# ScalarE's casts of sources and values behind the Gelu of the messages, and another order of small steps at the end of layer 0

## The chip, the cores and the metric

The kernel runs on one core of one Trainium2 chip. The metric is the device time of one execution in microseconds (us), the median of the runs given. TensorE is called PE here (PEld its weight load), VectorE DVE, ScalarE ACT, GpSimd POOL, and SyncE, which only issues DMAs, SP. A line number such as L1012 is a line of the kernel before.

## The reference

A graph of N = 2708 nodes with D = 128 features each passes through four layers; each takes h = relu(layernorm(x)) and adds its result to x. The adjacency matrix adj is 2708 x 2708 in f32, with about 0.6% of its entries not zero and the diagonal set.

- Layer 0: x + (adjᵀ h) / (column sums of adj).
- Layer 1: messages between nodes, `aggregated[i] = sum over j of gelu(s[i] + d[j] + msg_b) * adj[i, j]`, with s and d two linear images of h; then a dense update with a Gelu, and a layernorm.
- Layer 2: adj h through a linear map and a GRU cell.
- Layer 3: two heads of masked attention over adj's entries, with their own layernorms.

The change touches the end of layer 0 and layer 1.

## The kernel before

Nodes are cut into 22 tiles of 128 rows (NT = 22, the last one of 20 rows), and a matrix row into 22 blocks of 128 columns (NB = 22). Each engine works through its instructions in the order of the code: the order is written by hand, there is no planner. The kernel issues, for each part, a short function for one step of the work, and the order of the calls is what the change edits.

**Layer 0.** The matrix is read in pieces of 512 columns (a cut, `c`, 0 to 5; LAST is 5) by sets of four row tiles (`s`, 0 to 5). For each piece PE sums adjᵀ h, ACT and PE also turn the piece over for a later layer, and DVE lists, for each block of 128 columns of a row, its eight largest entries and where they are (`list_cut`, MAX8 and FIND_INDEX8 in L356 and L358). These lists, `val` and `col`, are the edges of layer 1. The columns of the last cut are done by parts between the sets of cut 4 (`PARTS`). Steps of the column sums of cut c-1 run during cut c (`next_steps`): `lift`, `spread`, `sum_rows`, `sum_squares`, `normal_rows` are generators, of which `work_cut` takes one step at a time between its matmuls. Behind them the rows of h for layer 1 are made: `turn_rows`, `destinations` (d by PE), `take_lead` and `split_rest` (d cut into three bf16 parts, d3, by ACT, DVE and POOL), `invert`, `add`, `measure`, `rows`.

**Layer 1.** It computes messages only for listed entries, at most 128 per block and row tile. For tile `t` and block b, PE makes the arguments of the Gelu by two sums of three bf16 matmuls each (`combine`, L1012 and L1016): a choice of source rows, `sel` (a 0/1 matrix), times the parts of s (s3), plus a choice of columns, `cols`, times d3. ACT applies Gelu to 4 blocks of p_m at once (`activate`, L1024; p_m has two buffers, g three), and PE sums the results into the rows of the tile with a third matrix, `put` (`gather`, L1037, f32). A tile is one `period(t)` of six steps, k = 0 to 5, with one combine and one activate each; gathers of 8 blocks at k = 3 and 5, and of the rest at k = 1 of the next period.

While tile t is computed, its successors are prepared:
- tile t + 3: `rank` (PE: where each row's entries begin), `spread_ends`, `lead_of` (ACT, L568: first bf16 part of the values, into `xb`), `select_rows` (DVE: sel), `describe_rest` (L946: the rest `v_r` on DVE, its cast on ACT, L572, the third part and two copies on POOL), `finish_rows` (DVE, L625: sel minus sel shifted by a DMA, `later`);
- tile t + 2: `fetch` (PE, L639), `place` (DVE: value and column of each listed entry), `find_rows` (DVE: `mine`, L601);
- tile t + 1: `pass_on` and `spread_columns` (two DMAs on SP), `columns` (DVE: cols, L973), `put_values` (POOL, eight blocks) and `put_more` (ACT, L965, the other fourteen blocks in parts).

In every even period before the last, the two source tiles that come next are made: `project` (PE), `add_bias` (DVE: sb, L728), `take_sources` (ACT, L568: first part of s), and `sources_rest` (L991: the rest `s_r` on DVE, its cast on ACT, L572, the third part on POOL, a Gelu and two scalings on ACT). `mix` and `update` do the dense part for groups of four tiles in between.

Period 0 takes its preparation from the lists `opening` and the `run` ahead of it. Buffers that the steps name: `hot` and `picked` are scratch tiles of one buffer each, `xb` has two, by the parity of t.

Of the kernel before, what the change touches and what calls it, by code (L numbers as in the profile page):

```python
# [20 lines left out]
F32 = mybir.dt.float32  # L21
# [9 lines left out]
P = 128  # L31
# [29 lines left out]
def listed_layers(ctx: ExitStack, tc: tile.TileContext, x, adj, w, out, flag):  # L61
# [204 lines left out]
    def sum_squares(g):  # L266
        t, k = GROUPS[g]
        for q in range(t, t + k):
            junk = pool.tile([P, D], F32, name="junk")
            nc.scalar.activation(  # L270
                junk, xs[:, q, :], AF.Square, bias=flat[:, 0, q : q + 1], accum_out=flat[:, 1, q : q + 1]
            )
            if q == t + k - 1:
                shift, ve, rstd, tmp = (flat[:, r, t : t + k] for r in range(4))
                nc.gpsimd.tensor_scalar(ve, ve, 1.0 / D, EPS, ALU.mult, ALU.add)
                nc.gpsimd.tensor_tensor(rstd, ve, minus_half[:, 0:k], ALU.pow)
                nc.gpsimd.tensor_tensor(tmp, rstd, rstd, ALU.mult)
                nc.gpsimd.tensor_tensor(tmp, tmp, ve, ALU.mult)
                nc.gpsimd.tensor_scalar(tmp, tmp, -0.5, 1.5, ALU.mult, ALU.add)
                nc.gpsimd.tensor_tensor(rstd, rstd, tmp, ALU.mult)  # L280
                nc.gpsimd.tensor_tensor(shift, shift, rstd, ALU.mult)
            yield
# [167 lines left out]
    def turn_sums(g):  # L450

        t, k = GROUPS[g]
        p = sums_p[g] = bank("p_s0")
        for q in range(k):
            m = size(t + q)
            nc.tensor.transpose(p[0:m, q * P : (q + 1) * P], sums_T[g][:, q * P : q * P + m], ident)
# [59 lines left out]
    def next_steps(c, s):  # L516

        off = 1 if c < LAST - 1 else 0
        stage = s - 1 - off
        if stage == -1:  # L520
            return lift(c - 1)
        if stage == 0:
            return spread(c - 1)
        if stage == 1:
            return sum_rows(c - 1)
        if stage == 2:
            return sum_squares(c - 1)
        if stage == 3:
            return normal_rows(h, c - 1)
        return last_destinations() if stage == 4 and c == LAST - 1 else ()  # L530

    def last_destinations():
        destinations(LAST - 2)
        yield
        pass_on(0)
        project(0)
        turn_sums(LAST)
        yield

    def list_last(n):  # L540
# [41 lines left out]

    def less_lead(t):
        dst, src = values_of(t)
        rest = state["x", t] = opener.tile([P, NB, S], F32, name="hot")
        nc.vector.tensor_tensor(rest, src, dst[0], ALU.subtract)

    def pass_rest(t):
# [144 lines left out]
    for i, (c, s) in enumerate(order):  # L733
        g0, gk = GROUPS[s]
        list_cut(c, s, g0)
        if i == 0:
            state["f", 0] = factors(*state.pop(("m", -1)))
            list_cut(c, s, g0 + 1)
            state["m", 1] = moments(tiles_of(xs, *GROUPS[1]), "n4")
            list_cut(c, s, g0 + 2)  # L740
            state["f", 1] = factors(*state.pop(("m", 1)))
            list_cut(c, s, g0 + 3)
        else:
            for n in range(g0 + 1, g0 + gk):
                if c > 0 and s == (2 if c < LAST - 1 else 1) and n == g0 + 1:
                    invert(c - 1)
                list_cut(c, s, n)
            if c == LAST - 1:
                for n in {0: range(FIRST), 1: range(FIRST, 4), 2: range(4, HELD), LAST: range(NT - 2, NT)}.get(s, ()):
                    list_last(n)  # L750
                if s == 0:
                    count_some(0, FIRST)
                if s == 1:
                    count_some(FIRST, 1)
        if i + 1 < len(order):
            mask_near(*order[i + 1])
        if i > BEHIND and i - 1 - BEHIND + RING < len(order):
            load_cut(*order[i - 1 - BEHIND + RING])
        for z in {(LAST - 2, 3): (0,), (LAST - 2, 4): (1,), (LAST - 2, 5): (2,), (LAST - 1, 0): (3,), (LAST - 1, 2): (4,), (LAST - 1, 3): (5,)}.get(
            (c, s), ()  # L760
        ):
            load_cut(LAST, z)
        if (c, s) == (LAST - 1, 2):
            shift_rows(0)
        if c > 0 and s == (2 if c < LAST - 1 else 1):
            turn_sums(c - 1)
        if (c, s) == (LAST - 1, LAST):
            turn_rows(LAST - 2)
        work_cut(c, s, first_steps(s) if c == 0 else next_steps(c, s))
        if c > 1 and s == 3:  # L770
            split_rest(c - 2)
        if (c, s) == (LAST - 1, 3):
            pass_rest(0)
        if c > 1 and s == 0:
            turn_rows(c - 2)
        if c > 1 and s == 1:
            destinations(c - 2)
        if c > 1 and s == 2:
            take_lead(c - 2)
        if c == LAST - 1:  # L780
            if s == 1:
                ranked = rank(0, FIRST, bank("p_r"))
            for z in PARTS.get(s, ()):
                mask_near(LAST, z)
                work_cut(LAST, z)
            if s == 1:
                nc.vector.tensor_copy(*ranked)
                spread_ends(0)
                select_rows(0)
                lead_of(*values_of(0))  # L790
            if s == 2:
                less_lead(0)
                finish_rows(0)
            if s == 3:
                for q in range(2):
                    fetch(0, q)
            if s == LAST - 1:
                place(0)
                lead_of(*values_of(2))
                less_lead(2)  # L800
                for _ in lift(LAST):
                    pass

        if (c, s) == (1, 2):
            nc.sync.dma_start(msg_wT, w["msg_wT"])
        if (c, s) == (2, 3):
            nc.sync.dma_start(msg_b, w["msg_b"].partition_broadcast(P))
            nc.gpsimd.tensor_copy(src_self[:, 0, :], msg_wT[:, 0, :])
            nc.gpsimd.tensor_tensor(src_self[:, 1, :], msg_wT[:, 0, :], msg_wT[:, 1, :], ALU.add)

    write_one()

    pass_rest(2)
    lead_of(*values_of(1))
    take_lead(LAST - 2, pool.tile([P, 4, D], F32, bufs=1, name="part_x"))
    add(LAST)
    measure(LAST)
    less_lead(1)
    add_bias(0, d_rest.rearrange("p (t c) d -> p t c d", t=2))
    spread_ends(1)  # L820
    split_rest(LAST - 2)
    for _ in lift(LAST - 1):
        pass
    turn_sums(LAST - 1)
    rows(LAST)
    pass_rest(1)
    ending.close()
    l0.close()

# [31 lines left out]
    with (  # L861
# [82 lines left out]
                    )  # L944

        def describe_rest(t):  # L946
            rest_of(*values_of(t), once.tile([P, NB, S], F32, name="v_r"))
            describe_columns(t)

        def put_values(t):  # L950

# [25 lines left out]
        def sources(k):  # L977

            sb = once.tile([P, 2, 2, D], F32, name="sb")
            if k not in projected:  # L980
                project(k)
            add_bias(k, sb)
            take_sources(k)

        def take_sources(k):

# [140 lines left out]
        def period(t, opening):  # L1127
# [6 lines left out]
            for k in range(GB):  # L1134
# [3 lines left out]
                if k == 0 and c and begun:  # L1138
                    pass_on(t + 1)
                    spread_columns(t + 1)  # L1140
                if k == 1 and a:
                    nc.vector.tensor_copy(*rank(t + 3, 1, rpool.tile([P, CH], F32, tag="r", name="p_r")))
                    spread_ends(t + 3)
                if k == 1 and last:
# [23 lines left out]
                if k == 2:  # L1168
                    if now and t % 2 == 0 and t + 2 < NT:
                        sources(t // 2 + 1)  # L1170
                    if a and begun:
                        select_rows(t + 3)
                        describe_rest(t + 3)
                    if now and t % 2 == 0 and t + 2 < NT:
                        sources_rest(t // 2 + 1)
                    if now and t + 4 < NT - 2:
                        count_rows(t + 4)
                if k == 1 and t == NT - 2:
                    check_lists()
                if k > 0 and c and begun:  # L1180
# [12 lines left out]
                if k == 4 and a and not begun:  # L1193
                    select_rows(t + 3)
                    describe_rest(t + 3)
                if k == (4 if begun else GB - 1) and a:
                    finish_rows(t + 3)
                if k in (0, 3):
# [24 lines left out]
        def take_pair(g):  # L1223
# [6 lines left out]
        )  # L1230
        opening = {
            1: ((turn_rows, 4), (fetch_both, 1), (select_rows, 2), (put_more, 0, 1)),
            2: ((destinations, 4), (put_more, 0, 2), (put_more, 0, 3), (place, 1), (take_lead, 4), (finish_rows, 2)),
            3: ((split_rest, 4), (pass_on, 1), (spread_columns, 1), (put_more, 0, 4), (put_more, 0, 5)),
            4: ((fetch_both, 2), (find_rows, 1), (put_values, 1)),
            5: ((place, 2),),
        }
# [880 lines left out]
```

## Time and profile before

| what | value |
|---|---|
| three runs | 983.99, 986.82, 988.04 us, median 986.82 |
| profiled execution | 986.58 us, span 984.8 us |
| mean granted TensorE clock of the profiled execution | 0.968 |
| PE, DVE, ACT, POOL busy (share of the span) | 93%, 81%, 54%, 45% |
| layer 0 | 0 to about 200 us |
| layer 1 | about 201 to 544 us |
| layers 2 and 3 | from there to the end |

Busy time is the time in which an engine executed something. The profile also tells what ended each idle time of an engine: `PE p_m L1012 <- ACT g L1024` says that PE, before the matmul of line 1012 that writes p_m, waited for ACT's instruction of line 1024. Times in the timeline count from the span's start.

### The profile page before, as it was taken

How to read it: one execution, taken by the hardware profiler on the slowest of the kernel's cores; microseconds unless marked ns; L12 is line 12 of the kernel's file. 1: busy time of each engine (PE TensorE's matmuls, PEld its weight loads, DVE VectorE, ACT ScalarE, POOL GpSimd, SP SyncE). 2: the span in 40 equal slices, each digit the busy share in tenths (PEclk: the TensorE clock that was granted, in tenths of full speed). 3: DMA queues.
4: the chain of work that ended last, by engine and by line, in shares of the span. 5: the costliest groups of instructions: out<-in, count | busy, mean ns of one | idle time of the engine just before them, and what ended most of it. 6: DMA issues, size and time to landing. Idle time of an engine off the chain costs nothing. (4 is left out here: it accounts for less than half of the span.)

```text
span 984.8 us, 21973 instructions
## 1 busy us (share of the span) xinstructions
PE 911.1 (93%) x7948; PEld 742.5 (75%) x7948; DVE 797.0 (81%) x2753; ACT 531.8 (54%) x1561; POOL 444.1 (45%) x524
## 2 busy tenths in 40 slices
PE   6799999768999999899999999999789999999983
PEld 3465556558999999898999444444678999999972
DVE  7999999788988989889674756566689877997793
ACT  5766776656666756676566123433222553655242
POOL 5402221369976787969765634444111300430132
PEclk9999999978999999999999899999899999999996
DMA  9899998325543434323215355564301674456000
GB/s 334 286 354 365 359 368 296 125 94 160 169 129 117 149 115 135 120 81 132 91 62 190 119 190 208 194 237 134 93 6 57 211 245 151 145 186 208 1 17 15
DMA packets 81736, 163.61 MB, mean 166 GB/s; under 512 B 9100, under 2 KB 27056, under 8 KB 81618
## 3 DMA queue, kind: packets, MB, share of 16 engines
q1 hardware_dynamic: 62518, 129.98, 40.8%
q10 hardware_dynamic: 19100, 32.13, 9.0%
q8 instruction: 64, 1.05, 0.5%
q14 instruction: 54, 0.44, 0.1%
HBM read 115.47 MB, written 30.87 MB: 149 GB/s over the span
## 5 line engine op out<-in xcount | busy, mean ns | idle before, releaser
L1327 PE MATMUL att<-hv,wt 128*128 128x129 f32 x1672 | 195.7, 278 | 7.9 <-DVE wt L1297 6.4
L956 POOL TENSOR_SCALAR put<-count,line,value 128x128 f32<-128x128 f32 x176 | 197.6, 1134 | 11.1 <-DVE value L673 10.4
L1327 PEld LDWEIGHTS att<-hv,wt 128*128 128x128 f32 x1672 | 191.9, 194 | 10.9 <-DVE wt L1297 8.9
L1016 PE MATMUL p_m<-d,cols 128*128 128x128 bf16 (+1 forms) x1452 | 162.6, 221 | 9.2 <-DVE cols L973 4.3
L1012 PE MATMUL p_m<-s,sel 128*128 128x128 bf16 x1452 | 162.4, 221 | 5.0 <-ACT g L1024 4.9
L1297 DVE SCALAR_TENSOR_TENSOR wt<-row,lift,mask 128x1024 f32<-128x1024 f32 (+1 forms) x132 | 138.8, 1083 | 22.2 <-PE att L1327 22.2
L121 POOL TENSOR_TENSOR n_r<-n_r,minus_half 128x4 f32<-128x4 f32 (+1 forms) x28 | 38.9, 1389 | 237.7 <-DVE n_r L120 236.0
L1037 PE MATMUL agg<-put,g 128*128 128x128 f32 (+1 forms) x968 | 126.8, 284 | 0.0
L1037 PEld LDWEIGHTS agg<-put,g 128*128 128x128 f32 x968 | 116.2, 196 | 2.4 <-issue 0.2
L388 PE MATMUL sums<-a,h 128*128 128x512 f32 x220 | 113.9, 613 | 1.6 <-ACT h L137 1.6
L1488 PE MATMUL p_agg<-a,hs 128*128 128x512 f32 (+2 forms) x264 | 108.8, 554 | 2.8 <-DMA a<-adjT 2.8
L1012 PEld LDWEIGHTS <-sel 128*128 128x128 bf16 x1452 | 103.9, 99 | 9.0 <-issue 8.3
L1016 PEld LDWEIGHTS <-cols 128*128 128x128 bf16 (+1 forms) x1452 | 101.9, 99 | 10.1 <-DVE cols L973 5.0
L1024 ACT ACTIVATE g<-p_m 128x512 f32<-128x512 f32 x132 | 72.7, 552 | 63.8 <-PE agg L1037 45.0
L403 PEld LDWEIGHTS p_T<-ident,a 128*128 128x128 f32 (+1 forms) x440 | 55.4, 144 | 60.7 <-issue 43.1
L965 ACT ACTIVATE put<-mine,value 128x128 f32<-128x128 bf16 x308 | 100.6, 392 | 0.0
L358 DVE FIND_INDEX8 col<-val,a 128x8 uint16<-128x128 f32 x327 | 91.6, 298 | 0.0
L410 ACT ACTIVATE aT<-p_T 128x512 f32<-128x512 f32 (+2 forms) x132 | 71.1, 541 | 27.5 <-PE p_T L403 26.6
L1488 PEld LDWEIGHTS p_agg<-a,hs 128*128 128x128 f32 (+1 forms) x264 | 47.5, 193 | 50.6 <-issue 46.3
L403 PE MATMUL p_T<-ident,a 128*128 128x128 f32 (+1 forms) x440 | 70.5, 281 | 11.9 <-DMA a<-in_adj 6.2
L1450 ACT ACTIVATE hs<-hs 128x1354 f32<-128x1354 f32 (+1 forms) x44 | 58.5, 1330 | 39.9 <-DMA hs<-in_adj 39.5
L356 DVE MAX8 val<-a 128x8 f32<-128x128 f32 x327 | 79.4, 289 | 0.0
(297 smaller groups left out, 1529.0 us busy)
## 6 DMA issues: line engine op xcount, KB each, us to landing
hs<-in_adj SPq DMA_DIRECT2D x42, 677.0 KB
adjT<-aT ACTq DMA_DIRECT2D x50, 512.0 KB
a<-adjT SPq DMA_DIRECT2D x20, 1280.0 KB
a<-in_adj SPq DMA_DIRECT2D x24, 1024.0 KB
spread<-passed SPq DMA_DIRECT2D x22, 704.0 KB
later<-sel SPq DMA_DIRECT2D x22, 616.0 KB
cols_a<-in_adj SPq DMA_DIRECT2D x11, 320.0 KB
row<-own_d ACTq DMA_DIRECT2D x10, 256.0 KB
```

The costliest lines, as they stand in the source:

```text
L356: nc.vector.max(val[0:m, n, b, :], v)
L358: nc.vector.max_index(col[0:m, n, b, :], val[0:m, n, b, :], v)
L388: nc.tensor.matmul(accs[c][:, 0:w], h0[0:m, n, :], a[0:m, n - g0, t0 * P - lo : t0 * P - lo + w], start=(n == 0), stop=(n == NT - 1),)
L403: nc.tensor.transpose(p[0:k, i * iw + q * P : i * iw + q * P + m], a[0:m, q, e : e + k], ident[0:m, 0:m])
L956: nc.gpsimd.tensor_scalar(st["put", 0][:, b, :], count, st["line"][:, b : b + 1], st["value"][:, b : b + 1], ALU.is_equal, ALU.mult,)
L965: nc.scalar.activation(st["put", 1][:, b - HP, :], st["mine"][:, b - HP, :], AF.Identity, scale=st["value"][:, b : b + 1])
L1012: nc.tensor.matmul(p[:, b - b0, :], st["sel"][:, b, :], s3[:, q, t % 2, :], start=(q == 0), stop=False)
L1016: nc.tensor.matmul(p[:, b - b0, :], st["cols"][0:kb, b, :], d3[0:kb, b, q, :], start=False, stop=(q == 2))
L1037: nc.tensor.matmul(agg, g[:, b - 4 * k, :], put, start=(b == 0), stop=False)
L1297: nc.vector.scalar_tensor_tensor(wt[:, 0:n], row[:, k, c : c + n], lift[:, j, k : k + 1], mask[:, j, c : c + n], op0=ALU.max, op1=ALU.mult,)
L1327: nc.tensor.matmul(banks[s // 3][:, s % 3, :], wt[:, q * P : (q + 1) * P], hv[:, j, k, :], start=(v < 2 and s // 3 not in touched), stop=( ...
L1488: nc.tensor.matmul(pa[:, 0:n], h[0:k, j, :], a[0:k, j - j0, 0:n], start=(j == 0), stop=(j == NT - 1))
```

## The change

All edits move steps; the arithmetic stays the same.

- Cut 4, the last that is read whole: tiles 0 to 3 of the last cut's list are listed and counted at set 0 (before: three there, the fourth at set 1), tile 4 is counted at set 2, and the rank of four tiles is computed at once (p_r of 88 columns instead of 66), so period 0 computes none. The remainder of the values of tile 0 (`pass_rest(0)`) is issued ahead of the squares in set 3 (before: behind that set). `project(0)` and the first casts of the values of tiles 2 and 1 (`lead_of`) are steps of set 4. `turn_rows` of cut 3 comes between the last two parts of the last cut, `destinations` of cut 3 and `pass_on(0)` ahead of set 5. `less_lead(2)`, `less_lead(1)`, `spread_ends(1)` and `add_bias(0)` come directly behind `place(0)`; the rest of tile 1 uses a part of the scratch tile `picked`. `pass_rest(2)`, `pass_rest(1)` and `turn_sums(LAST)` are steps of set 5.
- Period 0: `split_rest(4)` comes in step 2 and `finish_rows(2)` in step 3 (before: the other way round). `take_sources(1)` and `sources_rest(1)` come at the end of steps 3 and 4.
- All later periods: `describe_rest` does only the subtraction on DVE in step 2. The cast of the rest on ACT and POOL's three instructions (`pass_rest`) come in step 3, behind `activate(t, 3)`. In even periods `take_sources` comes in step 3 behind that Gelu (before: step 2), and `sources_rest`, with its subtraction on DVE, in step 4 behind `activate(t, 4)`, so on DVE behind `columns`, `place` and `find_rows` of step 3.

```diff
@@ next_steps
         if stage == 2:
-            return sum_squares(c - 1)
+            squares = sum_squares(c - 1)
+            return in_turn(in_order((pass_rest, 0)), squares) if c == LAST - 1 else squares
         if stage == 3:
-            return normal_rows(h, c - 1)
-        return last_destinations() if stage == 4 and c == LAST - 1 else ()
-
-    def last_destinations():
-        destinations(LAST - 2)
-        yield
-        pass_on(0)
-        project(0)
-        turn_sums(LAST)
+            last = c == LAST - 1
+            return in_turn(in_order((project, 0), (lead_of, *values_of(2)), (lead_of, *values_of(1))), normal_rows(h, c - 1)) if last else normal_rows(h, c - 1)
+        if stage == 4 and c == LAST - 1:
+            return in_order((pass_rest, 2), (pass_rest, 1), (turn_sums, LAST))
+        return ()
+
+    def in_order(*steps):
+
+        for step, *numbers in steps:
+            step(*numbers)
         yield
...
@@ less_lead
-        rest = state["x", t] = opener.tile([P, NB, S], F32, name="hot")
+        if t == 1:
+            rest = opener.tile([P, NB, 4, S], F32, name="picked").rearrange("p b q s -> p (b q s)")[:, 0 : NB * S]
+            rest = rest.rearrange("p (b s) -> p b s", s=S)
+        else:
+            rest = opener.tile([P, NB, S], F32, name="hot")
+        state["x", t] = rest
...
@@ the sets of layer 0
-                for n in {0: range(FIRST), 1: range(FIRST, 4), 2: range(4, HELD), LAST: range(NT - 2, NT)}.get(s, ()):
+                for n in {0: range(FIRST + 1), 2: range(4, HELD), LAST: range(NT - 2, NT)}.get(s, ()):
                     list_last(n)
                 if s == 0:
                     count_some(0, FIRST)
-                if s == 1:
                     count_some(FIRST, 1)
+                if s == 2:
+                    count_some(FIRST + 1, 1)
...
         if (c, s) == (LAST - 1, LAST):
-            turn_rows(LAST - 2)
+            destinations(LAST - 2)
+            pass_on(0)
         work_cut(c, s, first_steps(s) if c == 0 else next_steps(c, s))
...
-        if (c, s) == (LAST - 1, 3):
-            pass_rest(0)
...
-                ranked = rank(0, FIRST, bank("p_r"))
+                ranked = rank(0, FIRST + 1, bank("p_r"))
             for z in PARTS.get(s, ()):
                 mask_near(LAST, z)
                 work_cut(LAST, z)
+                if z == LAST - 1:
+                    turn_rows(LAST - 2)
...
                 place(0)
-                lead_of(*values_of(2))
                 less_lead(2)
+                less_lead(1)
+                spread_ends(1)
+                add_bias(0, d_rest.rearrange("p (t c) d -> p t c d", t=2))
...
-    pass_rest(2)
-    lead_of(*values_of(1))
     take_lead(LAST - 2, pool.tile([P, 4, D], F32, bufs=1, name="part_x"))
     add(LAST)
     measure(LAST)
-    less_lead(1)
-    add_bias(0, d_rest.rearrange("p (t c) d -> p t c d", t=2))
-    spread_ends(1)
     split_rest(LAST - 2)
...
-    pass_rest(1)
@@ layer 1
         def describe_rest(t):
-            rest_of(*values_of(t), once.tile([P, NB, S], F32, name="v_r"))
-            describe_columns(t)
+            dst, src = values_of(t)
+            rest = state["x", t] = once.tile([P, NB, S], F32, name="v_r")
+            nc.vector.tensor_tensor(rest, src, dst[0], ALU.subtract)
...
@@ sources
             add_bias(k, sb)
-            take_sources(k)
...
@@ period
+                if k == 1 and a and not begun:
+                    spread_ends(t + 3)
-                if k == 1 and a:
+                elif k == 1 and a:
...
-                    if now and t % 2 == 0 and t + 2 < NT:
-                        sources_rest(t // 2 + 1)
-                    if now and t + 4 < NT - 2:
+                    if now and begun and t + 4 < NT - 2:
                         count_rows(t + 4)
+                even = now and t % 2 == 0 and t + 2 < NT
+                if k == 3 and a and begun:
+                    pass_rest(t + 3)
+                if k == 3 and even:
+                    take_sources(t // 2 + 1)
+                if k == 4 and even:
+                    sources_rest(t // 2 + 1)
...
+                if k == GB - 1 and a and not begun:
+                    pass_rest(t + 3)
...
@@ opening
-            2: ((destinations, 4), (put_more, 0, 2), (put_more, 0, 3), (place, 1), (take_lead, 4), (finish_rows, 2)),
-            3: ((split_rest, 4), (pass_on, 1), (spread_columns, 1), (put_more, 0, 4), (put_more, 0, 5)),
+            2: ((destinations, 4), (put_more, 0, 2), (put_more, 0, 3), (place, 1), (take_lead, 4), (split_rest, 4)),
+            3: ((finish_rows, 2), (pass_on, 1), (spread_columns, 1), (put_more, 0, 4), (put_more, 0, 5)),
```

`in_turn` takes the steps of several generators one after the other.

## The prediction

> **What bounds the kernel now.** I read first where the two touched stretches lie, in the busy time of each engine by stretch (columns: start and end, length, busy us and instructions of PE, PEld, DVE, ACT, POOL, then granted TensorE clock, DMA share, GB/s):
>
> ```profile
> core 0: us, PE busy (x) PEld busy (x) DVE busy (x) ACT busy (x) POOL busy (x), PEclk, DMA share, GB/s
> 175.00:190.00 15.00, 11.40 (x77) 7.83 (x76) 10.24 (x57) 8.99 (x39) 5.94 (x18) 0.89 0.34 128
> 190.00:205.00 15.00, 8.87 (x39) 4.81 (x38) 12.76 (x49) 9.34 (x31) 5.47 (x10) 0.79 0.39 127
> 205.00:222.00 17.00, 13.11 (x176) 12.00 (x177) 14.62 (x26) 9.93 (x30) 13.01 (x13) 0.88 0.14 44
> 222.00:545.00 323.00, 314.17 (x4377) 305.07 (x4376) 265.90 (x782) 210.40 (x639) 245.68 (x255) 0.98 0.40 126
> 393.00:409.00 16.00, 13.51 (x183) 12.99 (x182) 15.42 (x54) 11.05 (x35) 15.61 (x16) 0.89 0.30 96
> ```
>
> From 222 to 545, layer 1's periods, PE is busy 97% of the time at a clock of 0.98: it bounds them, and only its waits can be saved. From 190 to 222 it isn't: there a chain through DVE sets the pace. Period 12 (393 to 409) is one of two that PE does not fill. The waits between 150 and 545 (who waited for what: total us, times, longest) name the causes:
>
> ```profile
> ACT xb L572 <- DVE v_r L571: 6.2, 5, 1.8
> ACT s L568 <- DVE sb L728: 5.0, 3, 2.8
> PE p_m L1012 <- ACT g L1024: 4.9, 4, 2.5
> PE y L639 <- POOL xb L581: 4.8, 1, 4.8
> DVE hot L586 <- ACT xb L568: 4.6, 1, 4.6
> PE p_m L1016 <- DVE cols L973: 4.3, 2, 3.5
> PE p_m L1016 <- ACT d L253: 2.6, 1, 2.6
> PE p_m L1016 <- POOL d L254: 2.4, 1, 2.4
> ```
>
> The timeline places them (start, us, engine, line, operation, count, idle time before it):
>
> ```profile
> 178.60 0.86 PE L639 MATMUL y<-xb,sel 128*128 128x37 bf16 x22 [4.76 <-POOL xb L581]
> ...
> 190.14 0.34 DVE L586 TENSOR_TENSOR hot<-val,xb 128x176 f32<-128x176 f32 x1 [4.56 <-ACT xb L568]
> ...
> 205.76 0.50 PE L1016 MATMUL p_m<-d,cols 128*128 128x128 bf16 x3 [3.51 <-DVE cols L973]
> ...
> 402.23 0.33 PE L1012 MATMUL p_m<-s,sel 128*128 128x128 bf16 x3 [2.49 <-ACT g L1024]
> ```
>
> ```profile
> 397.26 0.41 ACT L568 CAST s<-sb 128x256 bf16<-128x256 f32 x1 [1.52 <-DVE sb L728]
> 399.04 0.37 ACT L572 CAST xb<-v_r 128x176 bf16<-128x176 f32 x1 [1.38 <-DVE v_r L571]
> ...
> 403.26 1.08 DVE L601 TENSOR_TENSOR mine<-count_h,lead 128x1792 bf16<-128x1792 bf16 x1
> ```
>
> PE's 2.49 us are thus ACT's: its source and value casts stand in the queue ahead of the Gelu that would free p_m, and wait for DVE. The same wait is 1.64 us in period 16; the other two of the four are 0.8 together.
>
> **The Trainium skill.** "PSUM — Partial Sum Buffer", Engine vs sequencer instructions: the queues of ScalarE, VectorE and GpSimdE are strict FIFO. The trace agrees: the Gelu of 401.61 starts only after both casts that waited, though PE had filled its p_m by 396.6. "TensorE: Matmul & The Clock Gate", What's actually happening: the idle clock is half, after an idle window of about 3.4 us, and full speed returns after about 3.4 us of work. Here 2.49 us of waiting were enough: the 16 gather matmuls after it took 3.42 us against 2.00 us before it, and in period 16 3.26 us after 1.64 us. So each of these two waits costs some 1.5 us more; waits of 0.8 us elsewhere cost nothing more. "GPSIMD Engine Reference", 1. Specifications: its SBUF interface is shared with VectorE. The trace agrees: DVE's n_r operation at 196.57 took 1.11 us beside a POOL operation of 1.20 us, its like 0.16; in period 4 cols took 1.44 us against 0.94.
>
> **The change, part by part.** The sum is against the profiled execution, 986.58 us (span 984.8, 1.8 around it), 0.24 under the median of the three runs, 986.82.
>
> (1) Last two sets of layer 0. DVE gains work early: counting of tile 4 (0.24+0.34, about 0.53 in its stream), and takes list and count of tile 3 some 1.2 us earlier, which delays invert and what ACT and PE take from it (PE's p_r wait of 0.36 becomes about 1.5; neither is late for the end of the lists). DVE is busy without a gap from 145 to 185, so 0.53 us is a true cost: the lists end at 183.4, not 182.9. pass_rest(0) moves ahead, so fetch(0) loses its 4.76 us wait; as DVE reaches place(0) only at 183.4, this buys nothing by itself. What pays is behind place(0) (2.70 us, to 186.1): less_lead of 2 and 1, spread_ends(1) and add_bias follow at once (0.26+0.26+0.12+0.60, to 187.35), since ACT's two lead casts went before them. DVE's wait of 4.56 us goes, and one of 1.2 us for ACT's d. Then, from the rows' durations: near lists 1.03, part_x 0.61, invert to measure 2.39 (191.4), POOL's power and d 2.8 (194.2), sel(1) 1.57, s_r 0.64, invert(4) to n_r 3.76, pair 0.41, cols(0) 0.93: 201.5. It ended at 205.70: **4.2 us earlier**. POOL's queue could make it 3 (pass_rest(2) and (1), about 2 us of xb, are now ahead of the power), and 5 if DVE's 1.11 us beside POOL goes. pass_on(0)'s two DMAs leave at about 188 instead of 193.49; the spread lands far ahead of cols(0), so this costs and gains nothing. No DMA changes its place in SP's queue.
>
> (2) Period 0. split_rest(4) goes before finish_rows(2), so DVE no longer makes d's rest after a compare of 1.62 us that itself waited 1.46 for a DMA: PE's waits of 2.60 and 2.35 us for d go, 4.95 together. Fewer half-speed matmuls after them (gather 2.76 against 2.00, five blocks at 0.64 against 0.33) give about 2 more. But what is late next is cols(1): behind the moved steps it ends at about 220.7, while PE, 12 us ahead of its old 230.5 by this sum, would want it at 218.4: a wait of 2.3 and 1.5 of slow clock. From 230.5 to 222.3: **8.2 us in all for (1) and (2)**, 5.5 to 10.5 with the ends above and the DMA of later (4.95 us from issue) bearing on finish_rows(2).
>
> (3) Periods from 1 on. The casts of s and xb no longer stand before the Gelu of step 3, so the waits of 2.49 and 1.64 us, twice 1.5 us of slow clock and 0.1 us of the small ones go: **7.2 us**. But s_r (DVE) now stands behind cols, place and mine; ACT's s rest cast waits for it, and behind the cast, on ACT, are the source Gelu, two scales, three puts and the Gelu of step 5, which frees the p_m that PE needs in step 1 of the next period. After s_r: 0.03+0.31+0.44+0.60+0.88+0.38+0.06 = 2.70 us; 0.52 more in periods 6, 10, 14, 18 (update's Gelu L1088), 1.55 more in 12 and 16 (four hs rows of L137). s_r ends about where mine ended before, as its own 0.33 us goes from ahead of mine. Period 12: 404.1, so release at 408.3; PE without its old wait would be there at 408.01-2.49-1.5 = 404.0. That is a wait of 4.2 us, and 2.8 in 16 by the same sum. PE will have waited 2.5 us in earlier periods that DVE didn't, so I take 3.4 and 2.1. The others by the same sum, with DVE's 0.9 us beside POOL in periods 4 to 8 given back as POOL's xb and s parts move later: 0.5, 0.15, 0.65, 0.1, 1.15 for 2 to 10, 1.15 and 0.3 for 14 and 18. Together 9.5, and twice 1.5 of clock: 12.5. So the part **costs 5.3 us net** (1.7 if DVE runs ahead, 11 or more if POOL's contention only moves).
>
> POOL's and ACT's instruction counts hardly change (a rank matmul of 0.17 us and one cast go); both hide beside PE.
>
> Sum: 986.6 - 8.2 + 5.3 = **983.7 us**. Faster or slower means by over 0.5%, 4.9 us, about what a measurement of this kernel can tell from no change.
>
> **Rivals.** A: the periods gain too. If DVE, freed of POOL's traffic and of casts that it awaits, has mine ready 1.5 to 2 us sooner, periods 12 and 16 wait under 1.5 us and the clock holds: the waits left are some 3 us against 7.2, so -8.2-4.2 = -12.4, 974.2. For it: DVE is busy only 82% of layer 1. Against: in period 12 it is busy 15.42 of 16 us. B: slower, by one mechanism, ACT's Gelu of step 5 behind s_r with PE's clock. If DVE keeps its old times relative to PE, the waits are 0.8, 1.1, 1.7, 0.6, 1.4, 4.2, 1.4, 2.8, 0.6 = 14.6, and if five of them drop the clock, 7.5 more: 22.1-7.2 = +14.9, less 8.2: 993.3. It decides once the waits with their clock pass 15.4 us, for then the opening's gain is spent; for it, the wait of 1.64 us that halved the clock; against, no wait of 0.8 us did. C: the opening doesn't gain because cols(0) or cols(1) stays where it was (POOL's queue or the DMA of later holds sel): -3+5.3, 988.9.
>
> **How the numbers follow.** Likeliest case 0.45, of it 0.10 past -4.9 us; A 0.33; B 0.14, of it 0.02 within 4.9; C 0.08. Faster 0.10+0.33 = 0.43, same 0.35+0.02+0.08 = 0.45, slower 0.12. The likeliest case's own range is 979 to 988; to hold 8 in 10 the range reaches over most of A and towards B: 972.5 to 990.5.
>
> **What would show it.** In the profile after: DVE's less_lead with no wait and the first cols matmul of PE near 201.5; no PE wait for d L253 or L254, but one of about 2 us for cols(1); PE at period 1 some 8 us earlier; no wait of PE ahead of step 5 of periods 12 and 16, but waits of over 2 us for g in step 1 of 13 and 17, with ACT's s rest cast waiting for s_r right after mine. If those waits are absent, A holds and I was wrong on (3); if PE waits in most even periods with gathers of 3.3 us after them, B.

## The result: 0.4% slower, and the profile after

| kernel | median of runs | profiled execution (span) |
|---|---|---|
| before | 987.83 us (20 runs) | 986.58 us (984.8) |
| after | 992.05 us (20 runs) | 989.51 us (987.7) |

The ratio is 1.0036, with a 95% interval of 1.0018 to 1.0054. The time lies outside the range of the prediction, and on the other side of before than its 983.7 us.

The busy times of the stretches (the same columns as before the change) show PE less busy from 393 to 409, a stretch that now holds a new wait of 4.07 us, and POOL without a pause from 205 to 222:

```profile
190.00:205.00 15.00, 8.49 (x42) 4.95 (x42) 13.19 (x42) 8.51 (x24) 8.78 (x14) 0.68 0.45 126
205.00:222.00 17.00, 14.01 (x202) 13.05 (x202) 15.83 (x26) 14.15 (x46) 17.00 (x14) 0.98 0.41 136
222.00:545.00 323.00, 307.75 (x4319) 298.67 (x4319) 258.88 (x773) 204.65 (x617) 240.57 (x249) 0.99 0.38 121
393.00:409.00 16.00, 11.93 (x163) 11.57 (x161) 13.41 (x39) 9.95 (x30) 16.00 (x17) 0.94 0.23 67
```

The waits (150 to 550; lines of the new file, in which L1017, L1021, L1029 are the old L1012, L1016, L1024, L646 is L639 and L573, L574 are L571, L572 of the sources). PE's waits for d are gone, and so is DVE's 4.6 us wait for the first cast of the values at the end of layer 0; PE's for g have doubled, and ACT now waits for s_r:

```profile
ACT s L574 <- DVE s_r L573: 11.7, 10, 3.3
PE p_m L1017 <- ACT g L1029: 10.0, 9, 4.1
PE p_m L1021 <- DVE cols L979: 6.9, 3, 3.5
PE y L646 <- POOL xb L583: 2.8, 1, 2.8
```

The timeline of PE places them: the first cols of period 0 at 201.89 (205.76 before), a wait for cols(1), one for POOL's xb, and one for g in step 1 of period 13, shown in the fence after it:

```profile
201.89 0.50 PE L1021 MATMUL p_m<-d,cols 128*128 128x128 bf16 x3 [3.51 <-DVE cols L979]
...
222.01 0.34 PE L1021 MATMUL p_m<-d,cols 128*128 128x128 bf16 x3 [1.89 <-DVE cols L979]
229.26 0.43 PE L646 MATMUL y<-xb,sel 128*128 128x37 bf16 x11 [2.84 <-POOL xb L583]
```

The last of these waits, with what stands behind it on DVE and ACT (all engines, in order of time):

```profile
400.40 1.08 DVE L608 TENSOR_TENSOR mine<-count_h,lead 128x1792 bf16<-128x1792 bf16 x1
401.40 0.76 DVE L573 TENSOR_TENSOR s_r<-sb,s 128x256 f32<-128x256 f32 x1
402.19 0.41 ACT L574 CAST s<-s_r 128x256 bf16<-128x256 f32 x1 [3.35 <-DVE s_r L573]
...
404.43 1.63 ACT L137 ACTIVATE hs<-xs,n_r 128x128 f32<-128x128 f32 x4
405.96 0.36 ACT L1029 ACTIVATE g<-p_m 128x256 f32<-128x256 f32 x1
...
406.38 0.33 PE L1017 MATMUL p_m<-s,sel 128*128 128x128 bf16 x3 [4.07 <-ACT g L1029]
```

Where the time went is read from one mark per period, PE's turning of `where` (p_w), which comes in step 0. "After, second" is the profile of the same kernel run once more (e12 below; its layer 0 ended about 1.5 us later):

| mark | before | after | difference | after, second |
|---|---|---|---|---|
| period 1 | 231.87 | 223.19 | -8.7 | 224.75 |
| period 2 | 245.44 | 241.30 | -4.1 | 242.78 |
| period 12 | 389.22 | 387.64 | -1.6 | 389.40 |
| period 13 | 407.95 | 402.08 | -5.9 | 403.84 |
| period 14 | 423.32 | 423.31 | 0.0 | 425.06 |
| period 17 | 469.22 | 466.61 | -2.6 | 468.36 |
| period 18 | 484.58 | 484.58 | 0.0 | 489.21 |
| last messages | 539.26 | 540.31 | +1.05 | 543.94 |

Three things are seen. The opening's gain of 8.7 us is there at period 1, and half is gone one period later. Between periods 2 and 12 another 2.5 us go, in small waits. Periods 12 and 16 run without their old waits (the gains at 13 and 17), and 13 and 17 give it all back. The first profile had a mild period 17; the second is 3.6 us behind it at the last messages, though its start was only 1.5 behind. The rest of the first profile's 2.9 us, 1.85, lies in layers 2 and 3, where nothing was changed; from the last messages to the end the profiles of all kernels here take 445 to 448 us in no order with their edits, and the second profile of after takes 445.7, as before does (445.5).

### The profile page after: what moved, and what is told of

It is laid out like the page before. It is cut to its first block, busy times and chain, and to the rows that moved or that the text cites. A ratio compares the mean times of both kernels' runs of the same rounds, so it can differ in the third digit from the quotient of the medians.

```text
span 987.7 us, 21978 instructions
## 1 busy us (share of the span) xinstructions
PE 909.3 (92%) x7947; PEld 741.1 (75%) x7947; DVE 795.5 (81%) x2752; ACT 533.0 (54%) x1561; POOL 448.2 (45%) x524
## 3 DMA queue, kind: packets, MB, share of 16 engines
q8 instruction: 64, 1.05, 0.5%
## 5 line engine op out<-in xcount | busy, mean ns | idle before, releaser
L962 POOL TENSOR_SCALAR put<-count,line,value 128x128 f32<-128x128 f32 x176 | 188.9, 1087 | 1.0 <-DVE value L680 1.0
L1017 PE MATMUL p_m<-s,sel 128*128 128x128 bf16 x1452 | 161.9, 221 | 10.1 <-ACT g L1029 10.0
L1021 PE MATMUL p_m<-d,cols 128*128 128x128 bf16 (+1 forms) x1452 | 162.2, 221 | 6.9 <-DVE cols L979 6.9
L1017 PEld LDWEIGHTS <-sel 128*128 128x128 bf16 x1452 | 103.8, 99 | 12.3 <-issue 11.6
L1029 ACT ACTIVATE g<-p_m 128x512 f32<-128x512 f32 x132 | 73.2, 556 | 73.3 <-PE agg L1042 53.6
L1021 PEld LDWEIGHTS <-cols 128*128 128x128 bf16 (+1 forms) x1452 | 101.8, 99 | 9.8 <-DVE cols L979 7.5
```

Of the source, the lines that this page charges most:

```text
L962: nc.gpsimd.tensor_scalar(st["put", 0][:, b, :], count, st["line"][:, b : b + 1], st["value"][:, b : b + 1], ALU.is_equal, ALU.mult,)
L1017: nc.tensor.matmul(p[:, b - b0, :], st["sel"][:, b, :], s3[:, q, t % 2, :], start=(q == 0), stop=False)
L1021: nc.tensor.matmul(p[:, b - b0, :], st["cols"][0:kb, b, :], d3[0:kb, b, q, :], start=False, stop=(q == 2))
```

## The experiments

Theory 1: the source casts cost time, because ACT's second cast waits for s_r behind `mine` and holds up the Gelu of step 5. Theory 2: the loss comes from POOL in period 0. Theory 3: it lies in layers 2 and 3. All were measured beside the kernel before on the same chip; its medians there were 988.09 (e1 to e4), 987.46 (e5 to e8) and 986.87 us (e9 to e12). A difference between kernels of two such groups, or to after's 992.05, is therefore taken from how far each lies from its own before; after lies 4.2 us over it.

| label | what it is, against after | median us | ratio to before (95%) |
|---|---|---|---|
| e1_casts_only | before, with only the periods' casts changed | 997.80 | 1.0108 (1.0069 to 1.0147) |
| e2_opening_only | periods' casts as before | 983.49 | 0.9945 (0.9920 to 0.9969) |
| e3_rest_at_step5 | source rest in step 5 | 998.87 | 1.0126 (1.0095 to 1.0157) |
| e4_xb_between_puts | xb between POOL's puts | 989.99 | 1.0019 (1.0003 to 1.0035) |
| e5_s_r_early | s_r ahead of columns | 988.25 | 1.0021 (1.0009 to 1.0032) |
| e6_values_late_only | sources as before, values late | 983.17 | 0.9955 (0.9937 to 0.9973) |
| e7_old_split_order | finish_rows, split_rest as before | 992.14 | 1.0047 (1.0026 to 1.0069) |
| e8_s_r_early_and_xb | e5 and e4 | 983.12 | 0.9962 (0.9946 to 0.9978) |
| e9_values_late_and_xb | e6 and e4 | 977.98 | 0.9903 (0.9870 to 0.9935) |
| e10_s_r_as_before | s_r in step 2, its cast in step 3 | 977.67 | 0.9901 (0.9886 to 0.9917) |
| e11_both | e10 and e4 | 973.31 | 0.9860 (0.9844 to 0.9877) |
| e12_after_again | none | 990.72 | 1.0039 (1.0022 to 1.0056) |

### One part of the change alone

```diff
e1, against before, periods from 1 on: describe_rest without the cast, and
+                if k == 3 and a and begun:
+                    pass_rest(t + 3)
+                if k == 3 and even:
+                    take_sources(t // 2 + 1)
+                if k == 4 and even:
+                    sources_rest(t // 2 + 1)
```

> The kernel before, with only the casts of the periods from 1 on moved (value rests to step 3, source leads to step 3, source rests to step 4); layer 0 and period 0 as before. Theory 1 (the casts cost: the Gelu of step 5 stands behind s_r on ACT): about +5 us against before, PE waits of 4 and 2.4 us for g in step 1 of periods 13 and 17. Theory 2 (the order of the periods is harmless, the loss comes from period 0's POOL queue): no loss, 0 to -7 us, and no such waits. Theory 3 (the loss lies in layers 2 and 3, through shifted loads): layer 1 ends no later, the total is later.

Measured: +9.7 us (997.80 against 988.09). Its profile has the waits for g in step 1 of periods 13 and 17 of 4.08 and 4.47 us, and four of 0.4 to 0.7; layer 1 ends 9.3 us later, so the loss is made in the periods. Theories 2 and 3 fall as the cause of the whole; theory 1 holds, with twice its price (its interval is 6.8 to 14.5 us).

```diff
e2, against after, periods from 1 on: step 2 again
+                        if begun:
+                            take_sources(t // 2 + 1)
...
+                        pass_rest(t + 3)
+                    if begun and now and t % 2 == 0 and t + 2 < NT:
+                        sources_rest(t // 2 + 1)
```

> The kernel after, with the casts of the periods from 1 on back where they were before; layer 0 and period 0 as after. Theory 1: PE's start of period 1 about 8.7 us earlier, a wait of some 3 us for POOL's xb in period 1 that takes half of it back, so -4 us against before. Theory 2: no gain, 0 to +4 us. Theory 3: total later than layer 1's end tells.

Measured: -4.6 us against before, as theory 1 has it; PE waits 3.62 us for POOL's xb in period 1. With e1: -4.6 + 9.7 = +5.1, near the +4.2 of both together. Within their intervals the two parts add up, and the casts are the larger.

```diff
e6, against e2: without this line
-                        pass_rest(t + 3)
+                if k == 3 and a and begun:
+                    pass_rest(t + 3)
```

> The kernel after, with the casts and rests of the sources back in step 2 (as before) in the periods from 1 on; only the values' casts stay in step 3. Theory 1: the waits in step 1 of periods 13 and 17 go, as the source rests no longer stand behind mine; the old wait ahead of step 5 in periods 12 and 16 stays in part, since the s cast still waits for DVE ahead of the Gelu of step 3: 983 to 986. If the values' casts matter as well as the sources', it lies 1 to 4 us under the kernel with only the opening changed (983.5).

Measured: 983.17, as e2. So the values' casts by themselves cost and bring nothing that these intervals (2 us each way) can tell, and the periods' loss, 8.5 us between e6 and after, is that of the sources. The waits ahead of step 5 stayed, as expected (PE for g 6.6 us in all).

### The order around s_r

```diff
e3, against after
-                if k == 4 and even:
+                if k == (GB - 1 if begun else 4) and even:
                     sources_rest(t // 2 + 1)
```

> The kernel after, with the rests of the sources (s_r, its cast, the Gelu and scales of the sources) behind the Gelu of step 5 in the periods from 1 on, instead of behind that of step 4. Theory 1: the waits for g in step 1 of the odd periods (4.07, 2.44 and five of 0.2 to 0.8 us) and the half clock after two of them go: about -11 us against after, -8 against before. Theory 2: as after, within 2 us.

Measured: 998.87 us, 6.6 slower than after instead of 11 faster. The waits for g went, but another took their place:

```profile
346.53 0.42 DVE L573 TENSOR_TENSOR s_r<-sb,s 128x256 f32<-128x256 f32 x1
346.99 0.41 ACT L574 CAST s<-s_r 128x256 bf16<-128x256 f32 x1 [5.06 <-DVE s_r L573]
...
349.21 0.24 ACT L698 COPY where_T<-p_w 22x128 bf16<-22x128 bf16 x1
349.50 0.18 PE L553 MATMUL p_r<-rows_n,before 128*128 128x22 bf16 x1 [5.10 <-ACT where_T L698]
```

On DVE s_r came to stand behind finish_rows and update's five small operations as well, so ACT's cast waited 5.06 us. Behind it on ACT is now where_T, which empties p_w; p_r takes the same PSUM buffer, so PE waited 5.10 us for it, 14.7 in six periods. In both kernels ACT waits for s_r; what differs is the instruction caught behind that wait.

```diff
e5, against after: the subtraction of sources_rest apart, in step 3
                 if k == 3 and even:
                     take_sources(t // 2 + 1)
+                    if begun:
+                        less_sources(t // 2 + 1)
```

> The kernel after, with only DVE's subtraction s_r moved: in the periods from 1 on it stands in step 3 behind the cast that it needs and ahead of columns, place and find_rows; ACT's order is unchanged (cast, Gelu and scales of the sources still between the Gelus of steps 4 and 5). Theory 1a (DVE's order is the cause: ACT's cast waits 3.3 us for s_r at period 12): that wait goes, the 4.1 us and 2.4 to 4.5 us of PE in periods 13 and 17 fall below 1 us and with them the half clock: -10 to -12 us against after. Theory 1b (ACT's own work between the two Gelus is the cause, 2.7 to 4.3 us of it): the waits stay within 1 us of what they are, -0 to -2 us against after.

Measured: 988.25 us, 0.8 over before and so 3.4 faster than after by the medians (the intervals of the two ratios overlap): far from 1a's 10 to 12, and not the unchanged waits of 1b. ACT's wait for s_r is gone, but DVE now waits for ACT's first cast, which stands behind the Gelu of step 3, with columns, place and find_rows behind it (timeline of e5, period 14):

```profile
429.01 0.40 ACT L570 CAST s<-sb 128x256 bf16<-128x256 f32 x1
429.44 0.84 DVE L999 TENSOR_TENSOR s_r<-sb,s 128x256 f32<-128x256 f32 x1 [2.40 <-ACT s L570]
```

Such waits come to 15.7 us in nine even periods. PE, in turn, waits for where (1.0 us), for rows_n (3.1) and still 4.9 for g. The wait changed its engine.

```diff
e10, against after: less_sources and take_sources in step 2, and
-                if k == 4 and even:
+                if k == (3 if begun else 4) and even:
                     sources_rest(t // 2 + 1)
```

> The kernel after, with DVE's order in the periods from 1 on as before (source lead cast and s_r in step 2), and only ACT's second cast, Gelu and scales of the sources behind the Gelu of step 3. Theory 1: no wait in step 1 of periods 13 and 17, as the cast never waits for s_r, and no wait ahead of step 5 of periods 12 and 16, as less stands ahead of the Gelu of step 3: 976 to 981. If DVE's order alone decides, as with the values' casts late (983.2) within 1.5 us.

Measured: 977.67 us, as theory 1 has it: 9.2 under before and 13 under after (990.72 on the same chip, e12). In the periods from 1 on ACT no longer waits for s_r; DVE's waits for the first cast are six of 0.2 to 0.3 us, as before the change, since s_r and the cast that it needs stand where they stood, and only ACT's later work is behind the Gelu of step 3. In step 1 of periods 13 and 17, where theory 1 has no wait for g, 1.0 and 0.8 us are left. PE's waits in 222 to 545:

```profile
PE y L646 <- POOL xb L583: 2.8, 1, 2.8
PE p_r L553 <- DVE rows_n L880: 2.7, 2, 1.9
PE p_m L1025 <- ACT g L1037: 2.6, 4, 1.0
PE p_m L1029 <- DVE cols L979: 2.4, 2, 1.9
```

The nearest kernel is e6, which differs only in the place of ACT's second cast, Gelu and scales of the sources and of POOL's third part: e10 gains 4.9 us on it. The prediction had 7.2 for the waits that the casts had caused, before s_r's new place was counted.

### POOL in period 0

```diff
e4, against after
-            4: ((fetch_both, 2), (find_rows, 1), (put_values, 1)),
+            4: ((fetch_both, 2), (find_rows, 1), (put_values, 1, (0, HP // 2))),
...
                     describe_rest(t + 3)
-                if k == GB - 1 and a and not begun:
                     pass_rest(t + 3)
+                    put_values(t + 1, (HP // 2, HP))
```

> The kernel after, with POOL's eight puts of tile 1 in period 0 issued in two halves, and the rest of the values of tile 3 (xb) cast and passed between them. Theory 1: the 2.84 us wait of PE's y for POOL's xb in period 1 goes, with the slow clock after it: -4.5 us at the start of period 2; how much of it is left at the end of layer 1 depends on whether the later waits, set by DVE, take it back: -1 to -4.5 us against after. Theory 2 (all of the loss is here): back to before's time or under it.

Measured: 989.99 us, 1.9 over before where after is 4.2 over it; their intervals overlap, so that a gain is not told from none. In e4's profile the wait for xb is gone and period 2 starts at 236.89, 4.4 us earlier than in after's. At period 10 nothing of this is left (359.16 against 358.78):

```profile
319.49 0.95 DVE L980 TENSOR_SCALAR cols<-spread,part 128x2816 bf16<-128x2816 bf16 x1 [3.32 <-DMA spread<-passed]
...
342.23 0.33 PE L1018 MATMUL p_m<-s,sel 128*128 128x128 bf16 x3 [3.29 <-ACT g L1030]
```

In period 7 DVE waited 3.32 us for the DMA of spread (0.92 in after), so mine of period 8 came only 1.2 us earlier than in after, ACT waited 3.65 us for s_r there (1.62), and PE 3.29 us for g in period 9 (0.81), with 1.8 us of slow clock more. That PE was early isn't needed for this: in e7 below PE starts period 2 0.7 us later than in after, and its profile has the same chain (2.83, 3.67 and 3.06 us). Why the DMA lands later in some executions is not shown.

> Both: s_r early on DVE in the periods from 1 on, and xb of tile 3 between the two halves of POOL's puts in period 0. Theory 1a with the hidden gain: -12 us and another -4 us against after: 975 to 979. If DVE bounds the periods once PE's waits are gone, the second gain is given back, and it is within 1.5 us of the kernel with s_r early alone.

e8, both edits, measured 983.12 us, 5.1 under e5 alone on the same chip: with s_r early the gain is kept whole. The forecast of 975 to 979 was missed, as e5's was.

> The kernel with only the values' casts late (983.2) and xb of tile 3 between the two halves of POOL's puts in period 0. If the opening's second gain can be had when the source casts are not in the way: period 2 starts 4.4 us earlier, total 979 to 980. If DVE bounds the even periods from 8 on, as s_r's lateness with PE 4.4 us ahead suggests, at most half is kept: 981 to 983.

e9 measured 977.98 us, 8.9 under before where e6 is 4.3 under it: the gain is kept here too, though six runs tell it only to some 4 us. So DVE's work alone does not bound the periods. A late DMA need not cost anything either: in e10 DVE waits 2.67 us for spread in period 7, and PE waits for nothing in periods 8 and 9. In e4 it is s_r's place that let DVE's lateness reach PE.

The "previous kernel" of the next text is e10:

> The previous kernel with xb of tile 3 between the two halves of POOL's puts in period 0. Theory 1: 973 to 979, the fastest here. If DVE bounds the periods: within 2 us of the previous kernel.

e11, e10 with e4's edit, measured 973.31 us, 4.4 under e10 and the fastest here: 1.4% under before. The stretch from 222 to 545 (in e11 its last 14 us belong to layer 2) is PE's almost whole:

```profile
222.00:545.00 323.00, 316.90 (x4354) 301.40 (x4355) 267.61 (x801) 207.82 (x631) 254.86 (x257) 0.99 0.39 126
```

```diff
e7, against after
-            2: (..., (take_lead, 4), (split_rest, 4)),
-            3: ((finish_rows, 2), ...),
+            2: (..., (take_lead, 4), (finish_rows, 2)),
+            3: ((split_rest, 4), ...),
```

> The kernel after, with finish_rows(2) and split_rest(4) of period 0 in the old order. The prediction's part 2: PE waits again 2.6 and 2.4 us for d and period 1 starts some 4.5 us later. Theory of the hidden gain: PE's y of period 1 waits 2.8 us for POOL's xb in after anyway, so that wait shrinks and at most 1 us is lost at the start of period 2; the total is within 1.5 us of after (992).

Measured: 992.14 us, as after. The total is as the hidden gain has it, but the waits for d did not come back at all. ACT's cast of d in e7 started without a wait:

```profile
213.60 0.61 ACT L253 CAST d<-d_r 128x512 bf16<-128x512 f32 x1
```

In the kernel before it stood behind both casts, the Gelu and the scales of sources 1:

```profile
218.88 0.40 ACT L568 CAST s<-sb 128x256 bf16<-128x256 f32 x1 [2.83 <-DVE sb L728]
...
221.20 0.60 ACT L253 CAST d<-d_r 128x512 bf16<-128x512 f32 x1
```

They waited for sb, which DVE made only after finish_rows of tile 2 (216.62, 1.62 us, and 1.46 us of waiting for a DMA before it). After the change these steps stand behind d's cast, in steps 3 and 4 of period 0. That this move is what freed d is read from the two traces; no run takes it back alone.

### After once more

> The kernel after once more, for a second profiled execution. The same order of instructions: the wait in period 17, 2.44 us in the first profile and 4.47 in two kernels of the same order, shows whether it changes from one execution to the next; 4.5 would explain about 3 us between the first profile and the median.

Measured: 990.72 us. The wait in period 17 was 3.70 us this time, and the gather behind it ran at half clock, which it did not after 2.44 us in the first profile (first line after, other two e12):

```profile
470.64 1.58 PE L1042 MATMUL agg<-put,g 128*128 128x128 f32 x12
```

```profile
472.28 0.33 PE L1017 MATMUL p_m<-s,sel 128*128 128x128 bf16 x3 [3.70 <-ACT g L1029]
...
474.00 2.86 PE L1042 MATMUL agg<-put,g 128*128 128x128 f32 x12
```

Period 17 thus took 17.97 us in one execution of the same program and 20.85 in the other; e1 and e4 had 4.47 us there.

## Why the prediction was wrong

Two terms of the sum failed. The 8.2 us of (1) and (2) were taken as kept from period 1 on, with nothing for POOL's xb in period 1 (POOL was held to "hide beside PE"): that wait and its slow clock took back 4.5 us, and the opening is worth 4.6 us (e2; its interval is 3.1 to 7.9). And the 5.3 us of (3) were too small: it costs 8.8 us (after against e2).

**Part 1, layer 0: right.** DVE's wait of 4.56 us went, and that of 1.2 us too in the first profile (the second has 1.6); the first cols matmul came at 201.89, forecast near 201.5.

**Part 2, period 0: the sum was right up to period 1 and stopped one step too early.** Forecast 8.2 us earlier, with 2.3 us of waiting for cols(1); measured 8.7 and 1.89. (The terms given for PE add to 11.2 us, not to the 12 of the text; this changes nothing, since cols(1) sets the start.) But the step "what is late next is cols(1)" did not go on to POOL. This is POOL's queue after the change:

```profile
212.44 1.15 POOL L254 TENSOR_TENSOR d<-d_r,d 128x512 bf16<-128x512 f32 x1
213.59 12.58 POOL L962 TENSOR_SCALAR put<-count,line,value 128x128 f32<-128x128 f32 x8
226.13 2.08 POOL L575 TENSOR_TENSOR s<-s_r,s 128x256 bf16<-128x256 f32 x1
228.17 0.54 POOL L598 TENSOR_TENSOR xb<-v_r,xb 128x176 bf16<-128x176 f32 x1
```

xb of tile 3 stands behind the eight puts of tile 1 (12.58 us where they took 8.84 before: they ran beside five sel and mine operations of DVE, and beside two before) and behind s, which the change put there. It ended at 233.17+1.04 = 234.2 before and at 229.2 after: 5.0 us earlier, where PE came 8.7 us earlier. PE waited 2.84 us, and with the slow clock period 2 kept 4.1. The prediction named POOL's queue only as a bound ahead of period 1 and as rival C's reason, with a price that came from cols, not from xb. e2 measures the part at -4.6 us where the sum had -8.2; e4's period 2 start, and the 5.1 and 4.4 us that its edit gains in e8 and e11, show that the other half was POOL's. The cause given for the waits for d, the order of split_rest and finish_rows, was wrong too: split_rest has no instruction on DVE (take_lead subtracts), and e7 shows no wait without that edit.

**Part 3, the periods: right in mechanism, too small in size.** The waits ahead of step 5 in 12 and 16 went, and those in step 1 of 13 and 17 came, behind s_r and mine. For the nine even periods the sum had 9.5 us of waits; the first profile has 9.3 (periods 8 to 16 even: 0.81, 0.68, 4.07, 0.68, 2.44; 0.44 in 6 and 0.16 in 18), the second 11.0. With the clock loss that is 12.5 in the sum, 11.1 in the first profile, which has this loss only once, and 14.6 in the second; the old waits gave 7.7 back where the sum had 7.2. The values for periods 12 and 16 were lowered from 4.2 and 2.8 to 3.4 and 2.1 with the argument that PE's earlier waits would give DVE a lead: they came to 4.07, and 2.44 to 4.47. The half clock cost 1.8 us each, as forecast at 1.5 (period 13: 423.31-402.08 = 21.23 us against 15.37 before; 4.07 of it waiting), but in period 17 only in some executions. From period 2 to the last messages the part cost 5.2 us in the first profile and 7.3 in the second, against 5.3; in medians, 8.8 (after against e2) and 9.7 (e1 against before), each to some 3 or 4 us. The first profile's mild period 17 hides this. Why the medians are another 1 to 2 us above the second profile is not shown. A candidate is period 9, which took 16.3 us in both profiles of after but 20.4 and 20.2 in those of e4 and e7, whose order of the periods is the same.

**The sum**: +8.8 in place of +5.3, and -4.6 in place of -8.2. Either error alone would have brought the total to about before's; together they turn the sign. **Rival B** had the right side and the right mechanism, but not the extent: it wanted the half clock after five waits, there were one or two, and its threshold of 15.4 us of waits and clock was not passed (11.0 and 3.6, together 14.6, in the second profile). With an opening of 4.6 instead of 8.2 us the threshold is 11.8, and this was passed. That its 993.3 lies so near the measured time is luck: it has the periods' loss and the opening's gain both too large. **Rival C** named the wrong place: cols(0) and cols(1) came 3.9 and 6.8 us earlier. **Rival A** fell: mine began 1.3 us sooner after the start of periods 12 and 16 (12.8 us against 14.0, and 11.5 against 12.7), less than the 1.5 to 2 that it asks, and with s_r behind mine PE still waited 4.07 and 2.44 us.

The Trainium skill, "TensorE: Matmul & The Clock Gate", What's actually happening, has the window over which activity is judged run freely. The traces fit this: 1.83 us of waiting in period 13 of e5 halved the clock, 1.84 us at the same place in e8 did not, nor did 2.44 us in after. The idle window of about 3.4 us that it gives does not fit: 1.64 us were enough before the change.

## What to carry to other kernels

When an instruction is moved behind another on one engine, look also at what it waits for: its partner on the other engine (here s_r on DVE) was moved with it, behind 4.5 us of columns, place and find_rows (period 12 of after), and the wait went to whatever stands next in the first queue. Move only the part that was in the way (e10: the second cast and what follows), and leave the pair that feed each other where both are ready early. And follow a gain until an engine that had slack has none: a start 8.7 us earlier is worth no more than the fullest queue behind it allows, until that is reordered too (e8, e11).

## What the runs showed of the hardware

One wait of PE costs different amounts in different executions of one program: in period 17 of after, 2.44 us without a loss of clock, and 3.70 with 1.8 us more. Between 222 and 530 us of the 14 profiles, no wait of PE under 1.5 us lowered the clock, all from 3.2 us on did, and of those between 1.6 and 3.1 us some did and others not. One profile can so lie off the median: the first of after is 2.5 us under that of its 20 runs.

POOL's eight puts of 128x128 f32 for tile 1 took 1.1 us each before and 1.6 after. Those with one of DVE's cols, sel or mine operations beside most of them took 1.3 to 3.3 us, the others 0.8 to 0.9; after the change more of these operations fell into the time of the puts. No run moves the two apart, so this is seen together in time and not tested.
